# A four-layer graph network on one core: turned tiles that keep the graph as innermost index

## The chip, the cores and the metric

One core of a Trainium2 chip runs the whole kernel in one launch. The metric is the device time of one execution in microseconds (us); less is better. Before the change the median of three executions is 2754.69 us (2750.09 to 2756.34).

## The reference

There are 128 graphs, each of N = 128 nodes with D = 256 features, and an integer adjacency matrix `adj` of 128 x 128 for each. Four layers follow each other, each of the form `x = layernorm(x + layer(x, adj))`:

```
layer 0  e_k = leaky_relu((x * a_k) x^T), k = 0..3;  alpha = softmax(e_k where adj == k + 1, else -9e15)
         out = alpha x
layer 1  h = x W_msg;  out = relu(x W_upd + (adj^T h) / max(deg, 1) + bias)
layer 2  three steps: m = h W_i;  aggr = A^T m (A = adj != 0);  h = GRU(aggr, h)
layer 3  Wh = h W;  e = leaky_relu(Wh a1 + (Wh a2)^T), masked by adj > 0;  out = elu(softmax(e) Wh)
```

All data are float32.

## The kernel before

**Tiling.** Graphs are taken four at a time (`G = 4`), so there are 32 groups (`NG`). A tile with nodes on its 128 partitions has shape `[P, G, D]`; a turned tile has features on its partitions and the 512 nodes of the group (`T = G * N`) on its free dimension, one 128-feature half (`KC = 2`) at a time. Before the change the free index of a turned tile is (graph, node): the 128 nodes of graph 0, then those of graph 1.

**Stages of a group.** `loading`, `layer0`, `layer1`, `gru` (three times `step`) and `layer3`, the last four of which do the arithmetic. In `step`, `aggregate` multiplies the turned-back hidden state by the adjacency of each graph: 24 bf16 matmuls of 128 columns in each step, since the float32 state is written as the sum of three bf16 parts (`split`: the high half of `h`, the high half of `rest`, and what then remains). Its result goes into a PSUM bank `ps` and is copied to `agT`. Then four gates (`q`, `t_r`, `t_i`, `t_z`) are computed with seven products each instead of eight (`sums`, `gate`) from `hT` and `agT` by float32 matmuls of 256 columns. Each float32 matmul is two passes, and two rows, in the profile. The update makes the new hidden state in turned form, and it is turned back for the next aggregation.

**How tiles are turned.** [...] `turn` transposes all 32 x 32 blocks of a tile into `z`, and a write moves `z` to a DRAM buffer (`way_p` for the softmaxes, `way_1`, `way_2`, `way_h`, `way_3`, which the profile shows as `way` where the tag ends in a digit). `back` reads it again so that the blocks get to their places: four reads, one for each 32 partitions, in pieces of 32 floats. One block for this purpose is 128 x 512 floats, 256 KB. The tiles that come back are `probT` (layers 0 and 3), `x1T`, `hT`, `rT` (the same block as `hT`, read a second time at the last step), `hn` and `xc`. The first group, and the end of the last, use `turned_quick` instead: TensorE transposes through PSUM and a ScalarE copy.

**What sets the order of the work.** The kernel's functions only record operations. The planner at the end of the program issues them: for each of the five engines (PE, DVE, ACT, POOL and SP, whose only work is DMAs) it keeps a list of operations whose inputs are done, takes the engine that can start first, and on it the operation with the least nominal time. Nominal times come from `paced`: group `g` starts `PERIOD` later than group `g - 1`, the stages start and end as `TIMES` says, and `HEAD` and `TAIL` shift the first and the last six groups. When an operation ends is estimated by `pe_cost`, `dve_cost`, `act_cost`, `pool_cost` and `sp_cost`; a DMA lands after a time from the table `LANDING`. `holds` marks operations of VectorE and GpSimd that the planner does not let overlap. The engines then execute their lists in order, and wait on semaphores. So the recorded line of all operations is that of `issue` (L228 in the profile of before), and groups are told apart by tile names.

The shape of `back` before, which the change replaces:

```python
    def back(dst, way):
        for j in range(4):
            SP.dma_start(
                out=dst[j * 32 : (j + 1) * 32],
                in_=way[:, :, j * 32 : (j + 1) * 32].rearrange("n (i f) t -> f (n i) t", f=32),
            )
```

Of the kernel before, what the change touches and what calls it, by code (L numbers as in the profile page):

```python
# [18 lines left out]
def kernel(  # L19
# [133 lines left out]
    class Op:  # L153
        def __init__(self, engine):
            self.engine, self.calls, self.took, self.lasts, self.dma = engine, [], 0.0, 0.0, False
            self.after, self.bufs, self.waiting = {}, [], 0
            self.ready, self.nominal, self.urgent = 0.0, 0.0, False
            self.holds = False
            self.rush = 0.0

    class Engine:
# [24 lines left out]
        def __getattr__(self, name):  # L186
            def call(*args, **kw):
# [13 lines left out]
                op.dma = name == "dma_start"  # L201
                if self is POOL:
                    op.holds = name == "memset" or len(tensors) > 1
                elif self is DVE and name not in ("transpose", "bn_stats"):
                    op.holds = not any(v.buf.pool is psum for v in out + tensors) and (
                        len(tensors) > 1 or (name in FAST and m_of(out[0]) > 4)
                    )
# [28 lines left out]
    LANDING = {"e": 5.66, "adj_in": 4.0, "x_in": 3.85, "x1T": 3.53, "way_1": 3.2, "way_2": 3.0, "xc": 3.6, "way_f": 2.0}  # L236

    def tag_of(v):
        return v.buf.tag
# [20 lines left out]
    def act_cost(op, n, out, ins, pointers, sums):  # L260
        if op == "dma_start":
            return 0.6, 5.0
# [16 lines left out]
    def sp_cost(op, n, out, ins, pointers, sums):  # L279
        return 0.55, LANDING.get(tag_of(out[0]) if out else "out", 2.4)  # L280

# [8 lines left out]
    PERIOD = 81.83483  # L290
    EAGER, RUSH = 5.2365, 0.7497
    HOP, PE_HOP, SLACK, DMA_SLACK = 0.0946, 0.0838, 0.2615, 1.3152
    STAGES = ("loading", "layer0", "layer1", "step0", "step1", "step2", "layer3")
    TIMES = {
        "loading": ((-253.2780, -231.9501), (-180.9657, -182.6682),),
        "layer0": ((-168.5025, -107.0697),),
        "layer1": ((-62.6359, -4.7662),),
        "step0": ((-4.4948, 10.3141), (7.8309, 27.7350), (15.3585, 41.6638),),
        "step1": ((53.6280, 63.7962), (55.4424, 67.5800), (69.3938, 96.3237),),
        "step2": ((107.5318, 125.3405), (123.0192, 128.3402), (118.3669, 151.8864),),  # L300
        "layer3": ((179.8537, 241.5793),),
    }
    HEAD = (
        (-47.114, 18.617, -36.138, -28.741, -1.314, -6.344, -10.582),
        (24.334, 50.812, 17.569, -15.154, 21.237, -1.480, -6.111),
        (8.991, 0.482, 19.681, -1.325, -6.604, -1.406, -2.988),
        (-25.999, 20.490, 6.185, 5.893, -23.153, 10.547, -15.132),
        (-68.952, -1.643, -3.814, -2.005, -11.556, 1.656, 4.907),
        (153.035, -10.082, -1.797, 2.074, -6.131, -2.621, -1.970),
    )  # L310
    TAIL = (
        (-25.939, 2.926, -0.338, -2.915, -0.707, 12.085, 19.318),
        (-15.615, 8.572, 14.121, 0.973, -4.836, -7.460, 3.775),
        (16.695, 22.604, 4.276, 8.937, -5.182, 2.007, 1.764),
        (-11.456, -21.112, 0.381, -6.411, -11.631, 3.563, -8.765),
        (-90.353, -2.307, -9.971, -4.006, 15.211, 6.428, 6.000),
        (82.599, 6.878, -1.456, 4.198, -5.620, 19.044, 23.289),
# [162 lines left out]
    def turned(src, n, tag):  # L480

        way = tile_of(f"way_{tag}", [n, P, P], 8 if tag == "2" else 4, F32, dram)
        for first in range(0, n, G):
            turn(way[first : first + G], src[:, first : first + G])
        return way

    def turn(way, src):
        z = tile_of("z", [P, G, P], 4)[:, : src.shape[1]]
        DVE.transpose(z, src)
        SP.dma_start(out=way.rearrange("n p c -> p n c"), in_=z)  # L490

    def back(dst, way):
        for j in range(4):
            SP.dma_start(
                out=dst[j * 32 : (j + 1) * 32],
                in_=way[:, :, j * 32 : (j + 1) * 32].rearrange("n (i f) t -> f (n i) t", f=32),
            )

    def turned_quick(dst, blocks):

        ps = bank()
        with PE:
            for n, block in enumerate(blocks):
                PE.transpose(ps[:, n * P : (n + 1) * P], block, ident)
        ps = ps[:, : len(blocks) * P]
        if len(dst.shape) == 3:
            ps = ps.rearrange("p (n t) -> p n t", dst.shape, t=P)
        ACT.copy(dst, ps)

    def split(h, by):  # L510
# [3 lines left out]
        rest = tile_of("rest", [P, G, P], 4)  # L514
# [4 lines left out]
    def statistics(res, tag):  # L519
# [5 lines left out]
        for b in range(n):  # L525
            st = tile_of(f"st_{tag}", [P, 6], 4)
            DVE.bn_stats(st, res[:, b, :])
# [6 lines left out]
    def normalise(res, shift, rstd, quick):  # L534

        for b in range(res.shape[1]):
            if quick and b % 2 == 0:
                DVE.tensor_scalar(
                    res[:, b, :], res[:, b, :], rstd[:, b : b + 1], shift[:, b : b + 1],
                    op0=OP.mult, op1=OP.add,  # L540
                )
            else:
                ACT.activation(
                    res[:, b, :], res[:, b, :], AF.Identity, bias=shift[:, b : b + 1], scale=rstd[:, b : b + 1]
                )

    def softmax(alpha, tag, quick, tile=tile_of):
# [12 lines left out]
        pT = tile(f"probT_{tag[0]}", [P, n, N])  # L560
        if quick:
            turned_quick(pT.rearrange(FLAT), [alpha[:, b, :] for b in range(n)])
        else:
            back(pT.rearrange(FLAT), turned(alpha, n, "p"))
# [25 lines left out]
    def layer0(g, s):  # L590
# [39 lines left out]
        for h in range(G // 2):  # L630
            ps = bank()
            with PE:
                for j in range(2):
                    b = 2 * h + j
                    PE.matmul(ps[:, j * D : (j + 1) * D], pT[:, b, :], s.x[:, b, :], start=True, stop=True)
# [461 lines left out]
```

## Time and profile before

| | |
|---|---|
| median of three executions | 2754.69 us (2750.09 to 2756.34) |
| the profiled execution | 2750.87 us, of which 2749.0 us lie between its first and its last instruction (the span) |
| TensorE busy with matmuls | 2678.5 us, 97% of the span |
| TensorE weight loads (they overlap matmuls) | 2232.4 us, 81% |
| VectorE | 2183.6 us, 79% |
| ScalarE | 1807.6 us, 66% |
| GpSimd | 1570.5 us, 57% |
| granted TensorE clock, mean | 0.994 of full speed |
| DMA packets | 1,385,661, 288.37 MB |

The profile is of one execution. An engine's busy time counts its arithmetic; instructions that only issue DMAs, branch or wait are not counted. "PE" is matmuls and "PEld" weight loads; [...] the distance between the starts of two matmuls says more than the length of one. A view of stretches gives, for each, its length, then the busy time and number of instructions of PE, PEld, DVE, ACT and POOL, then the granted clock, the share of the DMA engines' time, and GB/s. A view of waits gives who waited for what: us in total, times, longest. A line on a DMA gives the destination and source, the number issued, KB of one, and the median us from issue to landing.

### The profile page before, as it was taken

The page shows a single profiled execution, that of the slowest core. Times are in us where ns is not written, and L with a number is a line of the kernel's source. Part 1 is how long each engine was busy: PE and PEld are TensorE (multiplying, and loading weights), DVE is VectorE, ACT ScalarE, POOL GpSimd, SP SyncE. Part 2 cuts the span into 40 slices and gives each one's busy share as a digit, 9 for nine tenths or more (in the row PEclk, how much of TensorE's full clock was granted, in tenths as well). Part 3 has the DMA queues.
Part 4 walks back from the last instruction along what each step waited for, and adds up shares of the span by engine and source line. Part 5 has one row for each costly group of instructions (what it writes and reads, how often), then busy time and mean ns, then how long its engine had stood idle before and what let it go on. Part 6 is the DMA issues. An engine that isn't in the chain of part 4 may idle for free. (4 is left out here: it accounts for less than half of the span.)

```text
span 2749.0 us, 45121 instructions
## 1 busy us (share of the span) xinstructions
PE 2678.5 (97%) x14332; PEld 2232.4 (81%) x14332; DVE 2183.6 (79%) x5044; ACT 1807.6 (66%) x4336; POOL 1570.5 (57%) x1546
## 2 busy tenths in 40 slices
PE   8999999999999999999999999999999999999995
PEld 5788888888888888888888888888887888887784
DVE  5777878778788877788878788878778888778875
ACT  3556666666666666766666676666766666666665
POOL 4555656555656555666555657555566555566542
PEclk9999999999999999999999999999999999999997
DMA  5545555545545555555555545555545546354432
GB/s 114 112 88 108 104 102 116 110 98 105 110 105 116 109 108 101 110 112 116 115 109 104 110 106 119 117 106 110 103 105 112 113 96 132 79 105 89 99 71 51
DMA packets 1385661, 288.37 MB, mean 105 GB/s; under 512 B 1139408, under 2 KB 1385296, under 8 KB 1385424
## 3 DMA queue, kind: packets, MB, share of 16 engines
q1 hardware_dynamic: 1382976, 283.13, 50.4%
q10 hardware_dynamic: 2448, 2.36, 0.3%
q8 instruction: 115, 1.88, 0.3%
q14 instruction: 122, 1.00, 0.1%
HBM read 168.96 MB, written 116.38 MB: 104 GB/s over the span
## 5 line engine op out<-in xcount | busy, mean ns | idle before, releaser
L228 POOL TENSOR_TENSOR t_r<-t_r,t_i 128x512 f32<-128x512 f32 x186 | 244.4, 1324 | 280.8 <-ACT t_i L228 207.5
L228 PE MATMUL gate<-t_h,w_hhT 128*128 128x256 f32 x1152 | 348.1, 386 | 5.9 <-ACT t_z L228 3.8
L228 PE MATMUL gate<-t_h,w_sh 128*128 128x256 f32 x1152 | 342.0, 383 | 4.1 <-ACT q L228 1.7
L228 PE MATMUL gate<-t_m,w_sm 128*128 128x256 f32 x1152 | 341.5, 380 | 1.0 <-DVE t_m L228 0.5
L228 PE MATMUL gate<-agT,c_gi 128*128 128x256 f32 x1152 | 340.3, 380 | 1.6 <-ACT t_z L228 0.6
L228 PE MATMUL gate<-t_m,c_gi 128*128 128x256 f32 x1152 | 340.4, 379 | 0.0
L228 PE MATMUL gate<-hT,w_hhT 128*128 128x256 f32 x1152 | 331.1, 382 | 3.9 <-ACT t_z L228 2.0
L228 POOL TENSOR_TENSOR t_d<-hT,t_n 128x512 f32<-128x512 f32 x192 | 250.8, 1319 | 45.1 <-ACT t_n L228 44.5
L228 PEld LDWEIGHTS gate<-t_h,w_hhT 128*128 128x128 f32 x1152 | 207.8, 190 | 63.8 <-issue 19.8
L228 PEld LDWEIGHTS ps<-xs,xT 128*128 128x128 f32 x2048 | 248.0, 192 | 13.4 <-ACT xs L228 3.7
L228 PE MATMUL ps<-xs,xT 128*128 128x128 f32 x2048 | 251.4, 275 | 2.6 <-ACT xs L228 1.2
L228 PEld LDWEIGHTS gate<-t_m,c_gi 128*128 128x128 f32 x1152 | 218.3, 190 | 39.3 <-issue 10.0
L228 PEld LDWEIGHTS gate<-t_h,w_sh 128*128 128x128 f32 x1152 | 208.4, 190 | 49.9 <-issue 13.8
L228 PEld LDWEIGHTS gate<-hT,w_hhT 128*128 128x128 f32 x1152 | 215.4, 190 | 39.1 <-ACT t_z L228 3.6
L228 PEld LDWEIGHTS gate<-agT,c_gi 128*128 128x128 f32 x1152 | 217.4, 190 | 34.4 <-ACT t_z L228 1.8
L228 PEld LDWEIGHTS gate<-t_m,w_sm 128*128 128x128 f32 x1152 | 217.7, 190 | 33.1 <-ACT t_i L228 1.7
L228 PE MATMUL ps<-w_um,x1T 128*128 128x512 f32 x512 | 239.7, 593 | 0.0
L228 ACT ACTIVATE q<-gate,bhn 128x256 f32<-128x256 f32 x384 | 183.7, 479 | 63.0 <-PE gate L228 60.1
L228 POOL TENSOR_SCALAR mk<-a_f 128x512 uint8<-128x512 f32 x128 | 201.2, 1579 | 38.3 <-DVE alpha L228 23.1
L228 ACT COPY t_r<-gate 128x256 f32<-128x256 f32 x288 | 107.5, 373 | 172.0 <-PE gate L228 171.1
L228 POOL MEMSET alpha<- 128x512 f32 x64 | 33.3, 520 | 324.9 <-ACT wh L228 196.4
L228 ACT COPY t_i<-gate 128x256 f32<-128x256 f32 x384 | 142.3, 371 | 110.1 <-PE gate L228 105.1
(185 smaller groups left out, 6715.1 us busy)
## 6 DMA issues: line engine op xcount, KB each, us to landing
way<-z SPq DMA_DIRECT2D x188, 256.0 KB, 2.4
way_h<-z SPq DMA_DIRECT2D x128, 256.0 KB, 2.4
hn<-way_h SPq DMA_DIRECT2D x512, 64.0 KB, 2.4
x_blocks<-in_x_dram SPq DMA_DIRECT2D x256, 64.0 KB, 2.5
x_in<-in_x_dram SPq DMA_DIRECT2D x32, 512.0 KB, 4.2
rT<-way SPq DMA_DIRECT2D x256, 64.0 KB, 2.4
way_p<-z SPq DMA_DIRECT2D x62, 256.0 KB, 2.5
probT<-way_p SPq DMA_DIRECT2D x248, 64.0 KB, 2.8
```

The source lines that it names most:

```text
L228: getattr(self.engine, name)(*[a.real() if isinstance(a, View) else a for a in args], **{k: a.real() if isinstance(a, View) else a for k, ...
```

## The change

A turned tile now has its free index as (node, graph): the four graphs' values of one node stand side by side. `turned` takes the place of `turned` and `turn`: the transposed blocks are written to `z` with the graph innermost, four writes of 32 partitions each move `z` to DRAM in pieces of 128 floats, and `back` is one read of 512 contiguous floats for each of 128 partitions. `x1T`, `x3` (the tile `xc`) and `hn` become `[.., 128, G]`; whoever uses one graph of such a tile takes every fourth element (`of_graph`), and so do the aggregation's matmuls when they write PSUM. `way_f`, through which layer 3 broadcasts a row, is written with only the 16 rows that are read again, so that its read is contiguous. The planner's cost of a DMA becomes a queue with a service time (`SERVED`, `service`) and a fixed part. An operation of VectorE or GpSimd may now wait for a lock without holding it (`waits`), by operation name (`PAIRS`). `PERIOD`, `EAGER`, `RUSH`, the hops and slacks, `TIMES`, `HEAD` and `TAIL` have new values.

```diff
-            self.engine, self.calls, self.took, self.lasts, self.dma = engine, [], 0.0, 0.0, False
+            self.engine, self.calls, self.took, self.lasts, self.queued, self.dma = engine, [], 0.0, 0.0, 0.0, False
...
-            self.holds = False
+            self.waits = self.holds = False
...
+                if op.dma:
+                    op.queued = 0.95 if self is ACT else service(out, ins)
+                two = name in PAIRS
                 if self is POOL:
-                    op.holds = name == "memset" or len(tensors) > 1
+                    op.waits, op.holds = True, name == "memset" or two
                 elif self is DVE and name not in ("transpose", "bn_stats"):
-                    op.holds = not any(v.buf.pool is psum for v in out + tensors) and (
-                        len(tensors) > 1 or (name in FAST and m_of(out[0]) > 4)
-                    )
+                    op.waits = op.holds = not in_psum(out + ins) and (two or name in FAST)
...
-    LANDING = {"e": 5.66, "adj_in": 4.0, "x_in": 3.85, "x1T": 3.53, "way_1": 3.2, "way_2": 3.0, "xc": 3.6, "way_f": 2.0}
...
+    PAIRS = ("tensor_tensor", "tensor_add", "tensor_sub", "tensor_mul", "scalar_tensor_tensor", "copy_predicated")
+    SERVED = {"e": 1.2, "adj_in": 1.6, "x_in": 1.6, "x_blocks": 0.53, "way_f": 0.2}
+
+    def service(out, ins):
+
+        tag = out[0].buf.tag if out else "out"
+        return 1.5 if tag == "out" else SERVED.get(tag, 0.22 if tag[:3] == "way" else 0.8)
...
     def sp_cost(op, n, out, ins, pointers, sums):
-        return 0.55, LANDING.get(tag_of(out[0]) if out else "out", 2.4)
+        return 0.5, 1.75 + service(out, ins)
...
-    PERIOD = 81.83483
-    EAGER, RUSH = 5.2365, 0.7497
-    HOP, PE_HOP, SLACK, DMA_SLACK = 0.0946, 0.0838, 0.2615, 1.3152
+    PERIOD = 81.86092
+    EAGER, RUSH = 5.2050, 0.9728
+    HOP, PE_HOP, SLACK, DMA_SLACK = 0.0940, 0.0792, 0.2618, 0.9645
...
-    def turned(src, n, tag):
-
-        way = tile_of(f"way_{tag}", [n, P, P], 8 if tag == "2" else 4, F32, dram)
-        for first in range(0, n, G):
-            turn(way[first : first + G], src[:, first : first + G])
+    def by_graph(v, n=G):
+
+        return v.rearrange("p (x b) -> p x b", [P, N, n], b=n)
+
+    def of_graph(v, b):
+
+        return v[:, :, b] if v.shape[1] == N else v[:, b]
+
+    def by_rows(v):
+
+        return v.rearrange("p b (j f) -> p j b f", [P, 4, v.shape[1], 32], j=4)
+
+    def by_columns(v):
+
+        return v.rearrange("p (j f) b -> p j b f", [P, 4, v.shape[2], 32], j=4)
+
+    def turned(dst, src, tag, bufs=4):
+
+        n = src.shape[2]
+        z = tile_of("z", [P, 4, 32, G], 4)[:, :, :, :n]
+        DVE.transpose(z.rearrange("p j f b -> p j b f", [P, 4, n, 32]), src)
+        way = tile_of(f"way_{tag}", [4, 32, 4, 32 * G], bufs, F32, dram)
+        for i in range(4):
+            SP.dma_start(
+                out=way[:, :, i].rearrange("j f x -> f j x", [32, 4, 32 * G]),
+                in_=z[i * 32 : (i + 1) * 32].rearrange("f j t b -> f j (t b)", [32, 4, 32 * G]),
+            )
+        if dst is not None:
+            back(dst, way)
         return way
 
-    def turn(way, src):
-        z = tile_of("z", [P, G, P], 4)[:, : src.shape[1]]
-        DVE.transpose(z, src)
-        SP.dma_start(out=way.rearrange("n p c -> p n c"), in_=z)
-
     def back(dst, way):
-        for j in range(4):
-            SP.dma_start(
-                out=dst[j * 32 : (j + 1) * 32],
-                in_=way[:, :, j * 32 : (j + 1) * 32].rearrange("n (i f) t -> f (n i) t", f=32),
-            )
+
+        SP.dma_start(
+            out=dst.rearrange("p x b -> p (x b)", [P, T]), in_=way.rearrange("j f i x -> (j f) (i x)", [P, T])
+        )
...
-        rest = tile_of("rest", [P, G, P], 4)
+        rest = tile_of("rest", h.shape, 4)
...
-                    PE.matmul(ps[:, j * D : (j + 1) * D], pT[:, b, :], s.x[:, b, :], start=True, stop=True)
+                    PE.matmul(ps[:, j * D : (j + 1) * D], of_graph(pT, b), s.x[:, b, :], start=True, stop=True)
...
-                    PE.matmul(ps, xT[:, b, c, :], w_um[:, c, :], start=(c == 0), stop=(c == KC - 1))
+                    PE.matmul(ps, of_graph(xT[:, c], b), w_um[:, c, :], start=(c == 0), stop=(c == KC - 1))
...
-                                ps[:, b * N : (b + 1) * N], parts[c][k][:, b, :], s.a_ne[:, b, :],
+                                of_graph(by_graph(ps), b), of_graph(parts[c][k], b), s.a_ne[:, b, :],
...
-        x3 = s.x3 if n == G else s.x3[:, first:last]
+        x3 = s.x3.rearrange("p d b -> p b d", [P, G, D])[:, first:last]
...
-                        ps[:, : 2 + D], s.rT[c][:, (first + b) * N : (first + b + 1) * N], w3x[:, c, :],
+                        ps[:, : 2 + D], of_graph(by_graph(s.rT[c]), first + b), w3x[:, c, :],
...
-            way = tile_of("way_f", [P, 32], 4, F32, dram)
-            SP.dma_start(out=way, in_=z)
-            SP.dma_start(out=f, in_=way.rearrange("(m r) c -> r m c", [8, 16, 32], r=8)[0].partition_broadcast(P))
+            way = tile_of("way_f", [16, 32], 4, F32, dram)
+            SP.dma_start(out=way, in_=z.rearrange("(m r) c -> r m c", [8, 16, 32], r=8)[0])
+            SP.dma_start(out=f, in_=way.partition_broadcast(P))
...
-        if op.holds:
+        if op.waits:
             at = max(at, (POOL if op.engine is DVE else DVE).held)
...
-        end = at + op.lasts + (DMA_SLACK if op.dma else 0.0)
+        end = at + op.lasts
+        if op.queued:
+            SP.held = max(at + 0.75, SP.held) + op.queued
+            end = SP.held + 1.0
+        if op.dma:
+            end += DMA_SLACK
```

## The prediction

> **What bounds the kernel now.** I read the busy line of the page first, then the busy time by stretch, then who keeps TensorE waiting.
>
> ```profile
> PE 2678.5 (97%) x14332; PEld 2232.4 (81%) x14332; DVE 2183.6 (79%) x5044; ACT 1807.6 (66%) x4336; POOL 1570.5 (57%) x1546
> ```
>
> The span is 2749.0 us, so TensorE is idle for 70.5 us in all. The stretches say where:
>
> ```profile
> 0.00:80.00 80.00, 65.21 (x341) 48.26 (x342) 48.38 (x125) 32.82 (x71) 40.67 (x49) 1.00 0.53 113
> 80.00:800.00 720.00, 706.79 (x3782) 585.60 (x3781) 572.45 (x1313) 466.05 (x1111) 414.78 (x407) 1.00 0.51 106
> 800.00:2000.00 1200.00, 1198.61 (x6503) 1013.82 (x6502) 973.26 (x2281) 820.97 (x1977) 702.89 (x697) 1.00 0.54 110
> 2000.00:2680.00 680.00, 666.72 (x3546) 555.50 (x3545) 549.51 (x1231) 451.72 (x1085) 395.05 (x378) 1.00 0.49 100
> 2680.00:2749.00 69.00, 41.20 (x166) 29.24 (x165) 39.97 (x98) 36.00 (x93) 17.09 (x17) 0.78 0.23 50
> ```
>
> The first number after the length is TensorE's busy time. From 800 to 2000 us it misses 1.4 us of 1200: nothing outside TensorE can save time there. The rest is 14.8 us at the start, 13.2 and 13.3 us in the two stretches beside the middle, and 27.8 us at the end, where the last graphs run down a serial chain. What ends the waits of TensorE:
>
> ```profile
> PE gate L228 <- ACT t_z L228: 7.9, 14, 1.5
> PE ps L228 <- DVE rest L228: 6.5, 7, 2.0
> PE ps L228 <- DVE rT L228: 6.1, 3, 3.7
> ...
> PE ps L228 <- DMA probT<-way_p: 1.2, 1, 1.2
> ```
>
> Only `rest` (made from a turned tile) and `probT` (a turned tile) hang on the transposes through DRAM: 7.7 us. The transfers themselves are many and small:
>
> ```profile
> DMA packets 1385661, 288.37 MB, mean 105 GB/s; under 512 B 1139408, under 2 KB 1385296, under 8 KB 1385424
> q1 hardware_dynamic: 1382976, 283.13, 50.4%
> way_h<-z SPq DMA_DIRECT2D x128, 256.0 KB, 2.4
> hn<-way_h SPq DMA_DIRECT2D x512, 64.0 KB, 2.4
> ```
>
> The engines of the DMA are busy half of the time, and hardly anything that TensorE needs is late for it.
>
> [...] weight loads last 99 ns for bf16 `rest` and 190 to 192 ns for fp32. [...]
>
> **The change, part by part.**
>
> *Transfers.* Before, a turned block of 256 KB is one write, and four reads in pieces of 128 B; after, four writes of 64 KB in pieces of 512 B and one read of 2 KB rows. There are 378 writes (188 + 128 + 62) and 440 blocks read back. DMAs on SP go from 378 + 1512 = 1890 (hn 512, rT 256, probT and hT 248 each, x1T and xc 124 each) to 4 x 378 + 440 = 1952: 62 more. Pieces of 128 B removed: 440 x 2048 = 901,120, and 31 x 2048 = 63,488 of the broadcast into `e`; added: (440 + 31) x 128 = 60,288 of 2 KB. About 480,000 packets remain. In the trace a 128 B packet takes 13.0 ns and one of 512 B 27.3 ns, so one of 2 KB some 105 ns (estimate, in proportion). Over 16 engines 964,608 x 13.0 / 16 = 784 us go and 60,288 x 105 / 16 = 396 us come: the share of 50.4% falls by 14 points, to some 36%.
>
> One round trip: before, in a quiet stretch, `way_h` was issued at 1060.77 and the last of four `hn` landed at 1067.18, 6.4 us. After: three issues of 0.38 us before the fourth write, which lands in 2.38 less 3/4 of the 512 x 27.3 / 16 = 0.87 us of its data, 1.7 us; then one read, 2.4 us less 512 x 13 / 16 = 0.42 us of data plus 128 x 105 / 16 = 0.84 us, 2.8 us. That is 1.1 + 1.7 + 2.8 = 5.6 us: 0.8 us less. SP is not the limit: (2316 + 62) issues of 0.49 us or less are under 1165 us of 2749. Behind a read that waits for its write stand other graphs' loads, as before; one read waits now instead of four. The gain on the path is at most the 7.7 us above, as these waits are up to 2.0 us long and a trip loses 0.8 us I take half: **-4 us**, bounds -8 and 0.
>
> *The plan.* The order of all engines is new: nominal times, a queue for SP in the costs of DMAs, and VectorE and GpSimd operations that wait for each other's lock. The counts of PE, DVE, ACT and POOL instructions do not change, and the matmul work is the same. The orders show one thing: the second use of the same `gate` bank within two matmuls of the first occurs 43 times before and 18 times after, each followed in the trace of before by some 70 ns of idle TensorE: 25 x 0.07 = 2 us. If the stretches at 80 to 800 and 2000 to 2680 ran like the middle (1.4 in 1200), 26.5 - 1.6 = 25 us would go; a plan worse by as much would add 25. I take **-4 us**, the 2 above and as much again from landings that come closer to what the plan assumes.
>
> *Strided weight loads.* x1T, rT and both probT (512 + 512 + 512 fp32 loads) and, in steps 1 and 2, hn and its two rests (1536 bf16 loads) are read 16 bytes apart. An fp32 load must fit beside a matmul pass that starts every 216 ns (256 columns; 429 ns for 512). `xs` passes start every 112 ns with loads of the same kind, so a load needs at most 112; doubled it would be 224, an excess of 8 ns on 1024 passes: 8 us at most. I take **0**, hidden under the streaming.
>
> *Strided writes to PSUM.* All 2304 matmuls of the aggregation write every fourth column. They are bf16 and start 56 ns apart:
>
> ```profile
> 1031.71 0.22 PE L228 MATMUL ps<-a_ne,hn 128*128 128x128 bf16 x1
> 1031.77 0.28 PE L228 MATMUL ps<-a_ne,rest 128*128 128x128 bf16 x2
> 1031.88 0.22 PE L228 MATMUL ps<-a_ne,hn 128*128 128x128 bf16 x1
> ```
>
> From 1031.77 to 1031.88 are two starts. Nothing hides this: TensorE is the bound. Bounds: 0, [...] and 2304 x 54 = +124 us, if each of 128 columns takes twice as long (56 to 110 ns); slower loads of bf16 weights lie inside the same bound. No reason gives a gain. I choose **0**, [...] while fp32 passes, of twice the time per column (216 ns for 256), cannot decide it; the other end is a rival.
>
> *Strided VectorE, ScalarE and GpSimd operands.* 378 transposes (259 us together, 0.69 us each) write 16 bytes apart; so do the copies of the last graphs, and xc's statistics and normalisation read so. Bounds: 0, and twice the time, +259 us on VectorE (79% to 89% busy). They lie beside TensorE's work; only what arrives late counts. I take **0**.
>
> Sum: 2750.87 (profiled execution: its span 2749.0 and 1.9 around it) - 4 - 4 = 2743. The median of three is 3.8 higher than that execution; half of this is added: **2745 us**, -0.35%. A difference of 0.2% (5.5 us) is about what a measurement can tell from none.
>
> **Rivals.**
> *A, as summed:* 2722 to 2749. For it: the idle stretches beside the middle, and the lighter queue. Against: only 7.7 us of waits name turned tiles.
> *B, no change:* 2749 to 2760. The transfers are hidden anyway, and the plan moves stalls about. For it: the middle stretch.
> *C, PSUM writes at half rate, slower:* the aggregation takes 2304 x 54 = 124 us more on a full TensorE: 2751 + 124 = 2875. It decides from the point where a strided matmul costs over 60 ns (4 x 2304 = 9 us, the gain). [...] Against: no measured factor.
> *D, late VectorE, slower:* transposes take up to twice as long, the in-order evictions behind them are late, and 5 to 10% of the 259 us (my estimate; all waits of TensorE for VectorE now are some 25 us) reach TensorE: +13 to +26, or a plan that fits worse by as much: 2764 to 2777. It takes over once a transpose lasts over 1 us.
> *E, the layout changes but the packets do not* (rows split again into small pieces): then B with four times the writes, 2750 to 2758.
>
> **Numbers.** A 0.40, B with E 0.13, C 0.20, D 0.27. So faster 0.40, same 0.13, slower 0.47. The likeliest, A, gives 2745. The range takes A, B and D with the bounds of the plan, 2722 to 2800, and leaves out C alone.
>
> **What would show it.** Right: the aggregation's matmuls still 56 ns apart, fp32 passes 216 ns, some 480,000 packets at a share near 36%, transposes still 0.69 us, the middle stretch full, and less idle time at 80 to 800 and 2000 to 2680. Wrong: starts 100 ns or more apart in the aggregation (C); transposes over 1 us and more waits of TensorE for VectorE (D); idle time in the side stretches grown with all durations unchanged (the plan).

## The result, and the profile after

The changed kernel takes 2922.09 us (median of four, 2919.98 to 2925.49) against 2755.52 us of the kernel before on the same chip: ratio **1.0609**, interval 1.0591 to 1.0628, slower by some 167 us. The profiled execution has a span of 2923.7 us and a granted clock of 0.993 of full speed, against 2749.0 and 0.994, so the clock plays no part. The busy line of the page:

```profile
PE 2835.2 (97%) x14332; PEld 2442.6 (84%) x14332; DVE 2324.4 (80%) x5044; ACT 1844.2 (63%) x4336; POOL 1605.2 (55%) x1546
```

The counts are those of before to the last instruction, and TensorE is again at 97%. It is busy for 157 us more with the same instructions: they have become slower. The timeline of TensorE in one aggregation (start in us, length in us):

```profile
1061.35 0.42 PE L229 MATMUL ps<-a_ne,rest 128*128 128x128 bf16 x2
1061.57 0.31 PE L229 MATMUL ps<-a_ne,hn 128*128 128x128 bf16 x1
1061.68 0.42 PE L229 MATMUL ps<-a_ne,rest 128*128 128x128 bf16 x2
```

From 1061.35 to 1061.57 are two starts: 110 ns for each, where it was 56 (the median over all of them is 109). The stretches of after (length, then busy time and instructions of PE, PEld, DVE, ACT and POOL, clock, DMA share, GB/s):

```profile
80.00:800.00 720.00, 705.09 (x3592) 610.82 (x3590) 577.10 (x1234) 447.79 (x1053) 390.52 (x378) 1.00 0.40 99
800.00:2000.00 1200.00, 1183.42 (x6051) 1024.96 (x6051) 966.40 (x2129) 777.80 (x1832) 686.40 (x659) 1.00 0.41 102
```

Two things are read here. In the same 1200 us TensorE gets through 6051 matmuls instead of 6503, while nearly as busy; and the middle stretch, which missed 1.4 us of 1200, now misses 16.6. The view of waits says on whom; the first two lines are from the kernel before, the others from after:

```profile
PE gate L228 <- DVE t_r L228: 2.3, 3, 1.2
PE gate L228 <- DVE q L228: 1.8, 3, 1.3
...
PE gate L229 <- DVE t_r L229: 15.8, 25, 1.3
PE gate L229 <- DVE q L229: 11.3, 14, 1.7
...
PE gate L229 <- ACT t_z L229: 4.8, 7, 1.4
...
PE ps L229 <- DVE rest L229: 2.4, 3, 1.2
...
PE ps L229 <- DMA probT<-way_p: 0.5, 1, 0.5
```

The waits on turned tiles (`rest`, `probT`) went down from 7.7 to 2.9 us, as the change would have it; the waits on VectorE's `t_r` and `q` went up from 4.1 to 27.1 us. Why VectorE is late is in the groups, whose second number after the bar is the mean length of one in ns. The first two are from the kernel before:

```profile
L228 PEld LDWEIGHTS <-rest 128*128 128x128 bf16 x1536 | 119.2, 99 | 28.8 <-DVE rest L228 9.0 <-issue 0.3 <-DVE fac L228 0.2
...
L228 DVE STREAM_TRANSPOSE z<-hT 128x512 f32<-128x512 f32 x128 | 89.9, 704 | 2.0
...
L229 PEld LDWEIGHTS <-rest 128*128 128x128 bf16 x1536 | 198.6, 154 | 18.5 <-DVE rest L229 3.9 <-issue 0.3
...
L229 DVE STREAM_TRANSPOSE z<-hT 128x512 f32<-128x512 f32 x128 | 144.2, 1133 | 0.5
...
L229 PEld LDWEIGHTS ps<-w3x,rT 128*128 128x128 f32 x512 | 129.6, 324 | 8.7 <-DVE rT L229 2.1 <-issue 1.6 <-PE gate L229 0.6
...
L229 DVE BATCH_NORM_STATS2 st<-xc 128x6 f32<-128x256 f32 x126 | 74.6, 619 | 14.3 <-DMA xc<-way_h 11.4 <-ACT xc L229 2.6
...
L229 DVE STREAM_TRANSPOSE z<-alpha 128x512 f32<-128x512 f32 x62 | 69.8, 1126 | 0.0
...
L229 DVE STREAM_TRANSPOSE xT<-x_blocks 128x512 f32<-128x512 f32 x64 | 44.6, 697 | 23.2 <-PE ps L229 14.6 <-DMA x_blocks<-in_x_dram 6.1 <-issue 1.3
```

What reads or writes the new layout an element at a time has stretched: fp32 weight loads from 191 to 324 ns, `bn_stats` (the statistics for layernorm) of `xc` from 407 to 619, transposes from 0.69 to 1.13 us. The bf16 loads of `rest` went from 99 to 154 on the mean, though only those of steps 1 and 2 are strided; runs 1 and 2 take this apart. The transpose of `x_blocks`, on which nothing was changed, still takes 0.70. The transfers, for which the layout was made, came out much as expected; page, DMA part:

```profile
DMA packets 478862, 287.92 MB, mean 98 GB/s; under 512 B 172320, under 2 KB 418208, under 8 KB 478624
...
q1 hardware_dynamic: 476176, 282.69, 38.6%
...
way_h<-z SPq DMA_DIRECT2D x760, 64.0 KB, 1.8
hn<-way_h SPq DMA_DIRECT2D x128, 256.0 KB, 2.9
```

**The sum.** To separate slower matmuls from waits I took the distance between the starts of each two consecutive matmuls from the trace. Up to 8 ns above the median of its kind it counts as streaming, the rest as gap. This is worked out from the matmul records, not shown by a view as such:

| | before | after | difference |
|---|---|---|---|
| aggregation, 2304 matmuls | 129.1 us (56 ns each) | 245.0 us (109 ns) | +115.9 |
| weights `rT`, 516 (4 of them with `agT`) | 112.8 us (218 ns) | 120.6 us (234 ns) | +7.8 |
| weights `probT`, 511 | 110.5 us (216 ns) | 119.5 us (233 ns) | +9.0 |
| all streaming | 2628.3 us | 2763.7 us | +135.4 |
| gaps | 104.1 us | 145.0 us | +40.9 |

The two last rows together are +176.3 us; the span grew by 174.7. Of the gaps, those before `gate` matmuls grew by some 38. Below, "streaming" and "gaps" are these two sums over the whole span.

### The profile page after: what moved, and what is told of

It is laid out like the page before. It is cut to its first block, busy times and chain, and to the rows that moved or that the text cites. A ratio compares the mean times of both kernels' runs of the same rounds, so it can differ in the third digit from the quotient of the medians.

```text
span 2923.7 us, 44906 instructions
## 1 busy us (share of the span) xinstructions
PE 2835.2 (97%) x14332; PEld 2442.6 (84%) x14332; DVE 2324.4 (80%) x5044; ACT 1844.2 (63%) x4336; POOL 1605.2 (55%) x1546
## 2 busy tenths in 40 slices
DMA packets 478862, 287.92 MB, mean 98 GB/s; under 512 B 172320, under 2 KB 418208, under 8 KB 478624
## 3 DMA queue, kind: packets, MB, share of 16 engines
q1 hardware_dynamic: 476176, 282.69, 38.6%
## 4 chain that ended last, share of the span: by engine, by line
PE 66%; DVE 18%; ACT 8%; issue 4%; DMA 3%; POOL 1%; SPq 1%; DVEq 0%; ACTq 0%; POOLq 0%
PE gate L229 40%; PE ps L229 25%; DVE z L229 4%; ACT xc L229 2%; DVE t_d L229 2%; DVE t_m L229 2%; DVE st L229 1%; DVE rest L229 1%; DMA x_in<-in_x_dram 1%; DVE q L229 1%; DVE rT L229 1%; DVE t_r L229 1%; DVE hT L229 1%; ACT agT L229 1%; ACT t_r L229 1%
## 5 line engine op out<-in xcount | busy, mean ns | idle before, releaser
L229 POOL TENSOR_TENSOR t_r<-t_r,t_i 128x512 f32<-128x512 f32 x186 | 251.2, 1360 | 267.6 <-ACT t_i L229 192.3
L229 PE MATMUL gate<-t_h,w_hhT 128*128 128x256 f32 x1152 | 342.0, 384 | 7.2 <-ACT t_z L229 4.5
L229 PE MATMUL ps<-a_ne,rest 128*128 128x128 bf16 x1536 | 270.2, 316 | 2.5 <-DVE rest L229 2.4
L229 POOL TENSOR_TENSOR rstd<-rstd,neg_half 128x4 f32<-128x4 f32 (+1 forms) x128 | 145.3, 1136 | 209.1 <-DVE rstd L229 200.2
L229 PEld LDWEIGHTS <-rest 128*128 128x128 bf16 x1536 | 198.6, 154 | 18.5 <-DVE rest L229 3.9
```

Of the source, the lines that this page charges most:

```text
L229: getattr(self.engine, name)(*[a.real() if isinstance(a, View) else a for a in args], **{k: a.real() if isinstance(a, View) else a for k, ...
```

## The experiments

The main theory: the aggregation's strided writes to PSUM double its time (rival C of the prediction), and late VectorE work makes the gaps (rival D). The rivals to it: that the strided bf16 loads (154 ns) set the pace of the aggregation, and that the new plan or the new transfers make the gaps. In runs 1 to 8, 12 and 13 elements of tiles land in, or are taken from, other places than the network wants, so nodes and graphs are mixed; the operations, their number and their sizes stay. Where medians are compared across chips, the ratios to the kernel before on the same chip are used.

**1. Only the writes to PSUM in order** (`a_psum_packed`)

```diff
-                                of_graph(by_graph(ps), b), of_graph(parts[c][k], b), s.a_ne[:, b, :],
+                                ps[:, b * N : (b + 1) * N], of_graph(parts[c][k], b), s.a_ne[:, b, :],
```

> The changed kernel, but the aggregation's matmuls write each graph's 128 columns of PSUM side by side instead of every fourth column; the weights stay 16 bytes apart. The columns then stand in another order than those of hT, so the state mixes nodes; no operation is added or left out. Theory 1 (writes to PSUM at half rate): starts of the aggregation's matmuls fall from 109 to 56 ns, 2304 x 53 = 122 us go, time near 2800 us. Theory 2 (the bf16 weight loads, 154 to 162 ns long instead of 99, set the pace): starts stay near 109 ns in steps 1 and 2 and only the 768 of step 0 speed up, time 2880 or more. Theory 3 (late VectorE and the new plan): starts change, but the time stays above 2880 as waits take their place.

Measured: 2834.39 us, ratio 1.0288 (1.0273 to 1.0303). The timeline of TensorE in this kernel:

```profile
1033.83 0.22 PE L229 MATMUL ps<-a_ne,hn 128*128 128x128 bf16 x1
1033.89 0.28 PE L229 MATMUL ps<-a_ne,rest 128*128 128x128 bf16 x2
...
L229 PEld LDWEIGHTS <-hn 128*128 128x128 bf16 x512 | 75.0, 146 | 2.8 <-issue 0.2
```

The starts are 60 ns apart (the median of steps 1 and 2), with the loads as strided as in after. Such a load lasts 146 ns here, where it was 162 in after and 99 before. Streaming fell by 107.9 us to 2655.8, but gaps rose by 18.7 to 163.7, 17 of it before gates: a faster TensorE waits longer there, for ScalarE (10.4 to 17.5 us) and for VectorE (30.4 to 33.9). That is why the time lies 34 us above the 2800 expected. So the writes cost about 108 us of streaming, of which 88 come back at once.

**2. Only the bf16 loads packed** (`a_parts_packed`)

```diff
+        if h.shape[1] == N:
+            h = h.rearrange("p x b -> p (x b)", [P, T]).rearrange("p (b x) -> p b x", [P, G, N], b=G)
         rest = tile_of("rest", h.shape, 4)
```

> The changed kernel, but the bf16 parts are taken so that a weight load reads elements 4 bytes apart, as before, instead of 16; writes to PSUM stay on every fourth column. The load takes other elements of the same tile. Theory 1 (PSUM): starts stay 109 ns and the time within 0.3% of the changed kernel, 2913 to 2931 us, though the loads' own length falls from 154-162 to about 99-129 ns. Theory 2 (loads): starts of the 1536 matmuls of steps 1 and 2 fall to 56 ns, 81 us go, time near 2840.

Measured: 2926.88 us, 1.0623 (1.0607 to 1.0639). The aggregation's timeline and its loads:

```profile
1000.45 0.31 PE L229 MATMUL ps<-a_ne,hn 128*128 128x128 bf16 x1
1000.56 0.42 PE L229 MATMUL ps<-a_ne,rest 128*128 128x128 bf16 x2
1000.78 0.31 PE L229 MATMUL ps<-a_ne,hn 128*128 128x128 bf16 x1
...
L229 PEld LDWEIGHTS <-hn 128*128 128x128 bf16 x512 | 67.4, 132 | 2.7
```

It stays at 109 ns. The loads do not set its pace; that rival falls. A load with no stride still lasts 132 ns beside matmuls that start every 109 ns, and 99 beside those of 56 ns in the kernel before: its recorded length is not set by its stride alone.

**3. The kernel before, with nothing but the strided writes** (`b_psum_strided`)

```diff
-                                ps[:, b * N : (b + 1) * N], parts[c][k][:, b, :], s.a_ne[:, b, :],
+                                ps.rearrange("p (x b) -> p x b", [P, N, G], b=G)[:, :, b], parts[c][k][:, b, :], s.a_ne[:, b, :],
```

> The kernel before, with one edit: the aggregation's matmuls write every fourth column of PSUM; who reads the bank reads it as before, so columns stand in another order. All else, plan and transfers too, is as before. Theory 1: starts rise from 56 to 109 ns, +122 us, time near 2875 us, perhaps some us more since the plan does not know it. Theory 2 or 3: under +15 us, time below 2770.

Measured: 2852.04 us, 1.0353 (1.0337 to 1.0368). The timeline:

```profile
1005.76 0.31 PE L228 MATMUL ps<-a_ne,xb 128*128 128x128 bf16 x1
1005.87 0.42 PE L228 MATMUL ps<-a_ne,rest 128*128 128x128 bf16 x2
1006.08 0.31 PE L228 MATMUL ps<-a_ne,xb 128*128 128x128 bf16 x1
```

109 ns from start to start by the median, streaming +115.4 to 2743.7, gaps -13.1 to 91.0, so the time is 23 us below the 2875 expected. The one edit makes +97 us in a kernel whose plan, transfers and VectorE are those of before. Together with run 1 this settles the aggregation.

**4. Only the fp32 loads of `probT`, `x1T` and `rT` packed** (`a_loads_packed`)

```diff
-                    PE.matmul(ps[:, j * D : (j + 1) * D], of_graph(pT, b), s.x[:, b, :], start=True, stop=True)
+                    PE.matmul(ps[:, j * D : (j + 1) * D], packed(pT, b), s.x[:, b, :], start=True, stop=True)
...
   (and so for xT[:, c], by_graph(s.rT[c]) and the probT of layer 3)
```

> The changed kernel, but the fp32 weight loads of probT, x1T and rT read 128 contiguous elements of the tile instead of every fourth (other elements of the same tile). Theory 1b (a strided fp32 load of 325 ns no longer fits beside a 256-column pass): starts fall from 234 to 216 ns on the 1024 passes of probT and rT, 18 us go, x1T's 429 ns stay, time near 2904 us. Rival (loads hidden, as predicted): within 5 us of 2922.

Measured: 2893.20 us, 1.0503 (1.0485 to 1.0520). Passes with `rT` and `probT` go back to 218 and 216 ns, streaming falls by 17.8 us, as expected, and gaps by 15.9, which was not expected and is not explained. `x1T` did not matter: 429 ns a pass in after too, with loads of 313 ns. So a strided load shows beside a pass of 256 columns and not beside one of 512.

**5. All of TensorE's accesses packed** (`a_pe_packed`: edits 1, 2 and 4)

> The changed kernel with every TensorE access packed: writes to PSUM, bf16 parts and fp32 weight loads all as contiguous as before (they take other elements of the same tiles, so nodes and graphs are mixed). What stays is the strided vector side, the new transfers and the new plan. The streaming of TensorE then returns from 2764 to 2628 us. Theory V or P alike: if the gaps between matmuls stay at 129 to 164 us as in the other variants, the time is 2628 + 145 + 20 = 2785 to 2800 us. Rival (the gaps are a consequence of the slow matmuls that the plan does not know): they fall back to the 104 us of before, time 2750 to 2760.

Measured: 2817.22 us, 1.0233 (1.0218 to 1.0249). Streaming is that of before again (2630.1), and all of the rest is gaps, 170.3, more than the 129 to 164 expected. The view of waits:

```profile
PE gate L229 <- DVE q L229: 17.1, 23, 1.2
PE gate L229 <- DVE t_r L229: 15.8, 25, 1.8
```

The remaining 2.3% is no matter of TensorE's own accesses.

**6. Transposes that write `z` in order** (`a_z_packed`)

```diff
-        DVE.transpose(z.rearrange("p j f b -> p j b f", [P, 4, n, 32]), src)
+        DVE.transpose(z.rearrange("p j f b -> p j (f b)", [P, 4, n * 32]).rearrange("p j (b f) -> p j b f", [P, 4, n, 32], b=n), src)
```

> The changed kernel, with one edit: the transposes write z in order (graphs are mixed with nodes in the turned tiles); all else stays. Theory V: 378 transposes fall from 1.13 to 0.69 us, TensorE's waits for VectorE fall from 40 us to under 20, and 15 to 35 us go: time 2887 to 2907. Theory P: the time stays within 8 us of 2922.

Measured: 2901.54 us, 1.0542 (1.0526 to 1.0558); gaps 122.4, 22.6 less than in after. Only half of the transposes answered. The groups of this kernel:

```profile
L229 DVE STREAM_TRANSPOSE z<-hT 128x512 f32<-128x512 f32 x128 | 140.6, 1103 | 0.5
...
L229 DVE STREAM_TRANSPOSE z<-alpha 128x512 f32<-128x512 f32 x62 | 42.7, 688 | 0.0
```

`alpha` is stored in order and is fast as soon as `z` is; `hT` is read with the graph innermost and stays at 1.10 us. One strided side costs nearly as much as two: 1.10 us for `hT` here, 1.13 for `alpha` in after, and 1.13 for `hT` there with both.

**7. PE packed, `z` written in order, `xc` read in order** (`a_all_packed`)

```diff
-        x3 = s.x3.rearrange("p d b -> p b d", [P, G, D])[:, first:last]
+        x3 = s.x3.rearrange("p d b -> p (d b)", [P, G * D]).rearrange("p (b d) -> p b d", [P, G, D], b=G)[:, first:last]
...
   (and the edits of 5 and 6)
```

> As the variant with all TensorE accesses packed, and the transposes write z in order, and layer 3 reads xc in order; only the new transfers and the new plan are left of the change (elements are mixed further). Theory V (gaps come from vector operations that last longer than the plan assumes, transposes 1.13 us instead of 0.69): transposes return to 0.69 us and the gaps to about 100 us, time 2735 to 2760. Theory P (the plan itself has the worse order): gaps stay over 130 us, time over 2780.

Measured: 2757.30 us, 1.0017 (1.0009 to 1.0024); gaps 113.9. From 5 this is 60 us less, in gaps alone: TensorE's own accesses are the same. The transposes of `hT` and `rT` are still at 1.10 us here, against the expectation; half of the transposes are at 0.69.

**8. No strided access left but in the few `turned_quick` copies** (`a_all2_packed`: 7, and `hT` and `rT` read in order by the transposes)

```diff
-  turned(turning[c], by_columns(by_graph(new[c])), "h")
+  turned(turning[c], new[c].rearrange("p (j b f) -> p j b f", [P, 4, G, 32], j=4, b=G), "h")
```

> As the variant with all accesses packed, and now also the 190 transposes that turn the hidden state back read it in order (elements are mixed, no work is left out). Only the new transfers and the new plan are left of the change. If these two are worth what the prediction said (-8 us), the time is 2743 us, 2735 to 2749; if they are worth nothing, 2750 to 2757; if the slow transposes were all that held the last variant back, its gaps of 114 us fall below the 104 us of before. All 378 transposes should last 0.69 us.

Measured: 2725.69 us, 0.9904 (0.9890 to 0.9917), 26 us faster than the kernel before. Its busy line and its middle stretch:

```profile
PE 2666.2 (98%) x14332; PEld 2228.0 (82%) x14332; DVE 2191.6 (81%) x5044; ACT 1807.5 (66%) x4336; POOL 1596.9 (59%) x1546
```

```profile
800.00:2000.00 1200.00, 1199.99 (x6517) 1012.78 (x6516) 995.55 (x2294) 821.36 (x1986) 727.33 (x702) 1.00 0.44 110
```

Transposes are at 0.69 us, streaming is 2627.6 and gaps are 78.1. The gain is three times the 8 us that was expected if the prediction's two terms held. This is what transfers and plan are worth with the price of the layout taken away; it is not a version of the kernel.

**9. The strides taken away from the aggregation's output while each element keeps its place** (`c_hT_blocks`): `hT`, `agT` and the gates are ordered (block of 32 nodes, graph, node), so a matmul writes four runs of 32 columns, and `rT` is made packed by four operations on VectorE instead of one.

```diff
-                                of_graph(by_graph(ps), b), of_graph(parts[c][k], b), s.a_ne[:, b, :],
+                                by_block(ps)[:, :, b], of_graph(parts[c][k], b),
+                                s.a_ne[:, b, :].rearrange("p (i t) -> p i t", [P, 4, 32], i=4),
```

> The changed kernel with another order of the free index in hT, agT and the gates: blocks of 32 nodes, graph, node in the block. The aggregation then writes PSUM in four runs of 32 contiguous columns, and hT still goes through DRAM in 512 B pieces and comes back in one read. The tiles that are only weights (probT, x1T, hn) and xc keep the graph innermost; the last update writes a copy for layer 3 with each graph's nodes contiguous, in four operations in place of one. Theory 1: runs of 32 contiguous columns cost nothing, so starts are 56 to 60 ns, 105 to 115 us go, and 9 us for rT: time 2800 to 2825. Rival (a write has to be contiguous over all 128 columns): starts stay over 100 ns, time over 2900.

Measured: 2853.55 us, 1.0369 (1.0353 to 1.0384): above what I expected. TensorE did its part. Its timeline in step 0, where the loads are not strided, has 50 to 60 ns from start to start; in steps 1 and 2 the median is 60, as in run 1:

```profile
1003.70 0.22 PE L229 MATMUL ps<-a_ne,xb 128*128 128x128 bf16 x1
1003.75 0.28 PE L229 MATMUL ps<-a_ne,rest 128*128 128x128 bf16 x2
1003.86 0.22 PE L229 MATMUL ps<-a_ne,xb 128*128 128x128 bf16 x1
```

Streaming is 2649.1, but gaps are 185.1, with VectorE at 2348.1 us. The waits (`t_z` 13.7, ScalarE's `q` 12.6, VectorE's `q` 11.2 us) fit a plan that does not know these operations; how much of the 185 is plan and how much load was not separated.

**10. The new planner and its constants over the old layout and transfers** (`b_new_plan`; its service times are those of the old transfers)

> The kernel before with its own layout and transfers, and with the new planner: lock, queue and all new constants and times; the service times are those of the old transfers by the trace of before (0.87 us for a write of 256 KB, 0.42 for a read of 64 KB, 0.84 for one of 128 KB). If the plan alone is worth something, 2735 to 2748 us and a faster version than both; if it fits the new transfers only, 2755 to 2775 us; between them no difference.

Measured: 2761.82 us, 1.0036 (1.0024 to 1.0049); gaps 114.6 against 104.1. The new plan by itself is no gain; it costs 10 us where the transfers are not those it was made for.

**11. Everything as in after, but the planner is told the real durations** (`a_costs`)

```diff
-  0.056 if split else 0.005 + m_of(out[0]) / 600.0
+  0.109 if split else 0.467 if any(v.buf.tag in ("rT", "probT_0", "probT_3") for v in ins) else 0.005 + m_of(out[0]) / 600.0
-            lasts = 0.17 + n * 0.00104
+            lasts = 0.17 + n * (0.00104 if ins[0].buf.tag in ("x_blocks", "wh") else 0.0019)
...
   (and bn_stats of xc 0.62 instead of 0.4, xc's normalisation +0.26)
```

> The changed kernel, with its planner told the durations that the trace of the changed kernel shows: 0.109 us for a matmul of the aggregation, 0.467 for the two passes on rT and probT, 0.17 + 0.0019 n for transposes, 0.62 for statistics of xc and 0.26 us more for its normalisation. Layout and work stay. Streaming stays at 2764 us; if the 41 us of new gaps come from a plan that does not know the durations, they shrink by 15 to 40 us: 2882 to 2907 us. If they come from VectorE being late whatever the order, the time stays within 10 us of 2922.

Measured: 2871.70 us, 1.0429 (1.0413 to 1.0445), 50 us less than after and 10 below the range expected. Streaming is as in after (2761.1), gaps fall from 145.0 to 100.6. The waits on `t_r` are nearly gone:

```profile
PE gate L229 <- DVE t_r L229: 4.3, 11, 0.9
...
PE gate L229 <- DVE q L229: 2.4, 5, 0.7
```

The engines here are as slow as in after, and VectorE's busy time (2354.1 us) is even higher. So most of what the gaps of after have over those of run 8 (145.0 against 78.1, at another pace of TensorE) came not from too much work for VectorE but from the order of the work: 44 of 67 us. The planner was told durations of TensorE and ScalarE too; which of them mattered was not separated.

**12. Step of two instead of four** (`b_psum_step2`: the kernel before, each matmul writing every second column, 8 bytes apart; two executions)

```diff
-  ps[:, b * N : (b + 1) * N]
+  ps.rearrange("p (h x b) -> p h x b", [P, 2, N, 2], h=2, b=2)[:, b // 2, :, b % 2]
```

> The kernel before, where the aggregation's matmuls write every second column of one half of the bank instead of every fourth column (8 bytes apart instead of 16; columns land in another order). If any step of more than one element halves the rate, starts are 109 ns and the time 2845 to 2855 us as with every fourth. If 8 bytes were still near enough, starts are 56 to 70 ns and the time under 2780 us.

Measured: 2850.93 us, 1.0361 (1.0342 to 1.0380), 109 ns per matmul as with step four. From 8 to 16 bytes the loss does not grow.

**13. No strided access, with the old constants** (`a_all2_old_times`: 8, its planner code included, with `PERIOD`, `TIMES`, `HEAD`, `TAIL` and their like of before)

> The variant with all accesses packed (elements mixed, no work left out), with the new planner code but the old constants: PERIOD, EAGER, RUSH, hops, slacks, TIMES, HEAD and TAIL of the kernel before. If the 26 us below the kernel before come from the transfers, the time stays at 2720 to 2735 us; if they come from constants that fit these transfers, it rises to 2745 to 2765 us.

Measured: 2760.14 us, 1.0022 (1.0013 to 1.0032); gaps 117.1 against 78.1 in 8. The second of the two expected cases came true. With run 10: new constants on old transfers cost 10 us, old constants on new transfers 6, and both new give 26. Which of the constants it is was not tried.

**14 and 15. Few reads, small pieces, no strides** (`d_small_writes`, and with the old constants `d_small_writes_old_times`): graphs outermost again; four writes of 64 KB in pieces of 128 B, four reads in rows of 2 KB.

```diff
+  way = tile_of(f"way_{tag}", [32, 4 * G, 4, 32], bufs, F32, dram)
+  SP.dma_start(out=way[:, :, i], in_=z[i * 32 : (i + 1) * 32].rearrange("f j b t -> f (j b) t", [32, 4 * G, 32]))
...
+  SP.dma_start(out=dst[j * 32 : (j + 1) * 32]..., in_=way[:, j * G : (j + 1) * G].rearrange("f b i t -> f (b i t)", [32, T]))
```

> The changed kernel with graphs outermost again, so no access of an engine is strided, and with another path through DRAM: four writes of 32 partitions in pieces of 128 B (z keeps the order of the transposes), then four reads of 2 KB rows. The planner is told 0.42 us of service for such a write and 0.22 for such a read; all constants are the new ones. If few and long reads are what helped, the gain stays: 2722 to 2740 us, faster than both kernels. If what helped was fewer packets in all, or one read in place of four, it is lost: 2750 to 2775 us.

> The same layout and path, with the old constants (PERIOD to TAIL). If the constants matter more than the path, this differs from its twin by 10 us or more, in the direction in which the packed variant moved; if not, both agree within 6 us.

Measured: 2923.40 us, 1.0612 (1.0596 to 1.0628), and 2912.42 us, 1.0574 (1.0558 to 1.0589). Both lie 137 us or more above everything expected, and the old constants are 11 us faster here, where they were slower in run 13. In the first, streaming is that of before (2632.0), and gaps are 266.9. Its longest wait, its chain that ended last by engine, and its DMA issues:

```profile
PE ps L229 <- DMA probT<-way_p: 57.1, 30, 3.8
```

```profile
PE 56%; DVE 14%; SPq 11%; DMA 7%; ACT 7%; issue 3%; POOL 2%; DVEq 0%; ACTq 0%; POOLq 0%
...
way_h<-z SPq DMA_DIRECT2D x760, 64.0 KB, 2.2
hn<-way_h SPq DMA_DIRECT2D x512, 64.0 KB, 2.0
```

One DMA lands no later than before (2.0 to 2.2 us against 2.4), but a block needs eight issues where the kernel before and after need five. They are also longer: by the medians of SP's records a write takes 0.63 us to issue and a read 0.42, where it was 0.38 and 0.49 before, 0.44 and 0.34 in after. That is 4.2 us of issuing for a block, against 2.3 before and 2.1 in after; all 3698 issues take 1935 us of the 2913, where 2378 take 1034 in after. SP then hardly waits for the transposes any more (the second line is run 14):

```profile
SPq L229 <- DVE z L229: 674.0, 120, 18.1
...
SPq L229 <- DVE z L229: 83.4, 42, 9.4
```

SP's queue, 1% of the chain in after, is 11% here, and the turned tiles come late. That the time of SP's issues is the cause is read from these views; no run took it away alone.

## Why the prediction was wrong

Two steps failed, worth some 90 to 100 us each: the terms for strided writes to PSUM and for strided operands of the other engines, which the sum put at 0.

- **Strided writes to PSUM: "I choose 0". This is the first step that failed.** The term's other end, +124 us, was nearly the truth: by the median 53 ns on each of 2304 matmuls, in sum +115.9 us of streaming in after and +115.4 in run 3. The text had the right bound, 56 to 110 ns for a matmul, and set it aside for a 0 that was an estimate with no measurement behind it. An unknown that lies wholly on the bounding engine (TensorE, 97% busy) should then have stood in the sum at its high end, not in a rival at 0.20. What the runs show: 109 ns at a step of four (run 3) and of two (run 12), and 56 to 60 with runs of 32 contiguous columns (run 9).
- **Strided operands of VectorE, ScalarE and GpSimd: 0. This is the second.** The transposes passed the mark that rival D named, over 1 us, on all 378 (1.13 us on the mean), and gaps grew by 40.9 us. Rival D had the mechanism, but its +13 to +26 was too small: with TensorE's accesses packed, the other engines' strides are worth 91 us (run 5 to run 8, by the ratios 1.0233 and 0.9904). Two things bear on the size. "They lie beside TensorE's work" leaves out that the plan must know how long they last: told the durations, the planner wins back 44 us of gaps (run 11). And what shows of late work depends on TensorE's pace: with all other engines unchanged, gaps rose by 18.7 us when TensorE became faster (run 1) and fell by 13.1 when it became slower (run 3).
- **Strided weight loads: 0, at most 8 us.** Measured +16.8 us by the table, 17.8 by run 4's streaming. The bound named the right passes, those of 256 columns and not those of 512 (429 ns before and after), but its size was not right: a pass of 256 columns went from 216 to 233 ns, where a doubled load of at most 112 ns gave 224. Two was a guess for the factor, not an upper end. The recorded length of a load (192 ns before, 325 after) does not give the pace either, since the `xs` passes start every 112 ns with loads of 192 ns. For bf16 the term holds nearly: 60 ns instead of 56, 8 us when the writes are in order (run 1), nothing behind the slow writes (run 2).
- **Transfers -4, plan -4.** With all strides gone the gain is 26 us (run 8). That is near the 25 us that the prediction gave as the plan's upper bound, and it comes in part from where that bound was read: from 80 to 800 us TensorE now misses 6.9 us instead of 13.2, and the middle stretch is full (1199.99 of 1200). It comes only from the new transfers and constants together; each without the other is a small loss (runs 10 and 13), so the two terms cannot be priced one by one. The packets were right (478,862 for 480,000; DMA share 38.6% for 36%; writes 1.8 us for 1.7, reads 2.9 for 2.8). SP's issues were read a little low: the 2316 of before take 1205 us by their records, 0.52 us each and not "0.49 us or less"; in after 2378 take 1034 us, so SP is still not the limit.
- **The addition of the cases.** A, C and D were held apart as alternatives, with a range that left out C. They do not exclude each other: what each of them named is in the result. In one order of undoing, in ratios times 2753 us: TensorE +104 (after to run 5, 1.0609 to 1.0233), the other engines +91 (run 5 to run 8), transfers and plan -26 (run 8 to the kernel before). They add up to the result by construction; another order would share it out otherwise. In after itself, with all else strided, `z` in order gives 18 us back (run 6) and the fp32 loads 29 (run 4).

Of the kernels in which every element is where the network wants it (after, and runs 9, 10, 11, 14 and 15) none is faster than the kernel before; the nearest, run 10, is at 1.0036. Whether a layout exists that keeps the 26 us of run 8 stays open.

## What to carry to other kernels

A layout that makes DMA pieces large was paid for here by every engine that then read or wrote an element at a time (a matmul of the aggregation 109 ns instead of 56, a transpose 1.13 us instead of 0.69, ScalarE's normalisation of `xc` 865 ns instead of 604, some 300 ns on GpSimd's `xd`): list all of those accesses, and put the unknown ones on the bounding engine at their high end. In what a bf16 matmul writes, runs of 32 contiguous elements were enough here (56 to 60 ns, run 9; shorter ones, from 2 on, were not tried); for a strided weight load, look at the pace of the passes, not at the load's own length (`rT`: pace 218 to 234 ns, load 191 to 324; `x1T`: pace 429 both times, load 190 to 313). When durations change, change the planner's costs with them, before judging what the work itself costs.

## What the runs showed of the hardware

- A bf16 matmul of 128 columns that writes fp32 PSUM columns 8 or 16 bytes apart starts every 109 ns instead of every 56 (runs 3 and 12); four runs of 32 contiguous columns cost nothing that shows (run 9: 56 ns in step 0, and 60 in steps 1 and 2, as with strided loads alone). No run has fp32 matmuls with strided output.
- A weight load of fp32 elements 16 bytes apart takes 313 to 326 ns instead of 190 to 192 (after against before). What shows in the pace: 233 to 234 ns instead of 216 to 218 at 256 columns, nothing at 512 (429 ns). In bf16 it takes 146 ns instead of 99 (run 1), and the pace goes from 56 to 60; beside the slow writes a packed load takes 132 (run 2) and a strided one 162.
- A transpose of 128 x 512 floats takes 0.69 us, 1.10 when its reads are strided (run 6), 1.13 when its writes are, and 1.13 with both: the factors do not multiply. `bn_stats` of `xc` went from 407 to 619 ns, ScalarE's normalisation of `xc` from 604 to 865. GpSimd's `xd` with `xc` went from 1320 to 1745, but it is at 1437 in run 8 with no stride left, so some 300 ns of this are the stride.
- From the DMA records: packets of 512 B took 36.3 ns on the mean in after, with its four smaller writes, and 27.3 before; those of 2 KB took 109.9. The prediction's 105 was called "in proportion", which from 27.3 would be 109.
